# Reordering TensorE's step lists in a transformer kernel of two branches

## The chip, the cores and the metric

The kernel runs on one core of one Trainium2 chip. The metric is the device time of one execution in microseconds (us); the figure for the kernel before is the median of three runs. A core has five engines with an instruction queue each: TensorE (PE in the profile; its weight loads are shown apart as PEld), VectorE (DVE), ScalarE (ACT), GpSimd (POOL) and SyncE (SP), which here issues the transfers. Each queue is worked off in the order in which it was written, and engines wait for each other through semaphores.

## The reference

The input x has 8 batches of 512 tokens with 128 features. It is layer-normalised once, and two branches work on the result; their sum is added to x.

```
x  = L0_attn_x                     # (8, 512, 128)
xn = _layernorm(x)
x  = x + attention(xn) + layers(xn)

attention: 16 heads of 8, causal, with a relative-position term of 5 rows for k and for v
layers:    for i in range(6):
               x = local_attn(shift_tokens(x)) + x
               x = ffn(shift_tokens(x)) + x

local_attn(x): q, k, v = split(x @ Wqkv)          # 16 heads of 64
               q, k = l2norm(q) * qs, l2norm(k) * ks, then rotary with a scale
               windows of 32: queries of a window see its keys and those of the window before
               softmax, then @ v, then @ Wo
ffn(x):        xn = layernorm(x) * g + b
               a, gate = split(xn @ W1 + b1)      # 2 x 341 columns
               a * gelu(gate) @ W2 + b2
```

## The kernel before

The first part, up to about 460 us of the profiled span, is the relative attention. The change does not touch it. The second part, from there to the end, is the six layers. It walks over 6 x 8 x 4 = 192 tiles of 128 tokens (layer, batch, quarter of the batch); n is a tile's number. A tile's place in its batch is called tile 0, 1, 2 or 3 below, and four tiles of one batch are a stretch.

Work on a tile is cut into named steps, which functions inside `steps_of_layers` emit. They are pipelined over tiles: while tile n has its scores made, tile n + 2 is projected and tile n - 1 is attended to.

- `p0` to `p3` (`project`, L776): a product of three matmuls (high and low halves of 32-bit numbers, L670 to L672) into `qk_ps`. VectorE multiplies it by the rotary cosine (L799) and sine (L800), ScalarE squares it (L801). After `p1` and `p3`, GpSimd adds the two rotary parts (L806). After `p1` it also adds the squares (L808), which VectorE sums per head (L809); after `p3` VectorE sums the squares directly (L811).
- `r` (`normalise`, L816): a chain of nine small VectorE instructions (L821, L75 to L86) on a tile `root_ps`, then GpSimd scales q and k (L826).
- `q0 q1 k0 k1` (`turn`, L840): four transposes each into `qkT_ps` (L845) and a ScalarE copy (L848).
- `s0 s1` (`scores`, L850): into two banks `sc_ps` a mask (L867) and 64 small matmuls (L879). VectorE takes two row maxima (L888), ScalarE eight exponentials (L892). After `s1`, VectorE inverts the sums (L904), GpSimd scales the probabilities (L905) and VectorE turns them into `pT` (L907).
- `v0` to `v3` (`values`, L912): a product into `v_ps`, a ScalarE copy (L921) and four transfers on SP's queue (L923).
- `a0 a1` (`attend`, L928): small matmuls into `y_ps` (L941), and after `a1` a ScalarE copy `ys` (L952). `+` (`add`, L955) turns `ys` and VectorE adds it to the stream `xt` (L962).
- `f`: one piece of the feed-forward of a batch that is complete. A stretch holds nine: split and mean (L976) in tile 1 after `+`, variance in tile 2, `rstd` in tile 3, then in the next tile 0 the three gate products with three Gelu activations (L1032) and three value products (L1042), and in the next tile 1 the last product `f_ps` (L1054), which VectorE adds to `xt` (L1066).
- `w1 w2`: pieces of the next layer's joint v and output weights. They do something only in tiles 2 and 3 of a layer's last batch.

The order of TensorE's instructions is written by hand: the strings of `ORDERS` (L49 to L54), one for each place in the batch, are read word by word (L1162). On the other engines the framework's scheduler sets a fixed order when the program is built, from its own estimates of times. So a change of `ORDERS` can also change the fixed order of the other four queues.

All products, turnings and the small chains take their PSUM tiles from one pool of six banks (`ps_x`, L1128). The scores have two banks of their own. A step that is given a bank waits until the step that had it before has been read out. Which bank a step gets is fixed at build time too. Exponentials and Gelu belong to different activation tables, so that each stretch has two table loads on ScalarE.

Of the kernel before, what the change touches and what calls it, by code (L numbers as in the profile page):

```python
# [46 lines left out]


ORDERS = (  # L49
    "p0 p1 v0 f s0 w2 + p2 f p3 q0 f f q1 s1 w2 k0 v1 w1 a0 r a1 w1 k1 v2 v3",  # L50
    "p0 s0 w2 p1 p2 v0 q0 f p3 f + f q1 s1 w2 k0 v1 w1 a0 r a1 w1 k1 v2 v3 f",
    "p0 p1 s0 w2 v0 v1 f p2 q0 q1 p3 s1 w2 k0 w1 + a0 r a1 w1 k1 v2 v3",
    "p0 p1 s0 w2 v0 f p2 q0 + q1 p3 v1 s1 w2 k0 w1 a0 r a1 w1 k1 v2 v3",
)  # L54


# [1230 lines left out]
```

## Time and profile before

| | |
|---|---|
| median of three runs | 3420.91 us (3416.99 to 3425.21) |
| profiled execution, its own time | 3422.36 us |
| span of the profiled execution | 3420.6 us |
| TensorE clock granted, mean | 0.992 |
| busy share PE / DVE / ACT / POOL | 94% / 88% / 81% / 80% |
| exponentials L892, without their accumulator reads | 3072, mean 348 ns |
| rotary products L799 and L800 | 768 each, mean 681 and 678 ns |
| table loads on ScalarE (L1032 and L892) | 47 and 46, mean 1283 ns |

The busy share of TensorE is from modelled ends of pipelined matmuls, so it is no proof that TensorE sets the time. The last column of a group's line tells how long the engine stood idle before these instructions, and what ended the wait. In a timeline, a line has the start, the duration, the engine, the line of the kernel, what is written and read, and in brackets the idle time before it with what ended it.

### The profile page before, as it was taken

Reading aid. Unit: us, or ns where it says so; the run is one execution under the profiler, and the core shown is the slowest. Engines: PE = TensorE matmul, PEld = TensorE weight load, DVE = VectorE, ACT = ScalarE, POOL = GpSimd, SP = SyncE. Lnnn points to the kernel's source line nnn. Section 1 sums busy time; section 2 is a strip of 40 time slices with the busy share of each in tenths; the row PEclk is TensorE's granted clock in tenths of the full one; section 3 lists DMA queues with packets and bytes.
Section 4 is the critical chain, followed back from the end, with each engine's and each line's share of the span. In section 5 each row is a group of like instructions: output and inputs, shape, how many; then the busy total and the mean of one; then the engine's idle time right before and its main releaser. Section 6 shows DMA issues by size and latency. Waiting matters only on the chain.

```text
span 3420.6 us, 132912 instructions
## 1 busy us (share of the span) xinstructions
PE 3207.7 (94%) x51264; PEld 2394.4 (70%) x51264; DVE 2998.4 (88%) x7542; ACT 2783.2 (81%) x9786; POOL 2752.1 (80%) x2102
## 2 busy tenths in 40 slices
PE   7999979999999999999999999999999999999997
PEld 4667657777777777667777767777767777776775
DVE  7777788999999999899898998989999898998994
ACT  5777768888888888888888888888888888887884
POOL 6767668888888888788888888888888887887883
PEclk9999999999999999999999999999999999999998
DMA  2111123332333323333233332323333233332332
GB/s 59 37 40 46 48 72 74 75 73 72 89 82 78 74 71 79 84 87 75 69 75 78 83 87 69 77 70 86 82 80 76 69 78 77 81 80 75 83 75 58
DMA packets 221067, 250.07 MB, mean 73 GB/s; under 512 B 73238, under 2 KB 115604, under 8 KB 220436
## 3 DMA queue, kind: packets, MB, share of 16 engines
q1 hardware_dynamic: 220148, 241.18, 28.4%
q8 instruction: 407, 6.67, 0.9%
q14 instruction: 224, 1.84, 0.2%
q10 hardware_dynamic: 288, 0.39, 0.1%
HBM read 26.92 MB, written 4.19 MB: 9 GB/s over the span
## 4 chain that ended last, share of the span: by engine, by line
PE 43%; DVE 27%; ACT 18%; issue 4%; DMA 3%; POOL 3%; SPq 2%; ACTq 0%; POOLq 0%; DVEq 0%
ACT pr L892 8%; PE y_ps L941 8%; PE qkT_ps L845 6%; PE sc_ps L879 4%; DVE q L799 4%; DVE rot L800 4%; PE f_ps L1054 3%; PE v_ps L670 2%; PE v_ps L671 2%; PE v_ps L672 2%; ACT sq L801 2%; DVE pT L907 2%; DVE mx L888 2%; PE qk_ps L670 2%; ACT L892 2%
## 5 line engine op out<-in xcount | busy, mean ns | idle before, releaser
L892 ACT ACTIVATE pr<-sc_ps,mx 128x64 f32<-128x64 f32 x3072 | 923.4, 348 | 96.9 <-DVE mx L888 92.6
L806 POOL TENSOR_TENSOR q<-q,rot 128x1024 f32<-128x1024 f32 x380 | 924.8, 2434 | 91.8 <-DVE rot L800 62.9
L826 POOL TENSOR_TENSOR q<-q,rn 128x1024 f32<-128x1024 f32 x380 | 717.4, 1909 | 4.1 <-DVE rn L86 3.8
L892 ACT ACTIVATION_READ_ACCUMULATOR pr<-sc_ps,mx 128x1 f32 x3072 | 719.5, 241 | 0.0
L801 ACT ACTIVATE sq<-qk_ps 128x512 f32<-128x512 f32 x768 | 469.7, 633 | 262.1 <-DVE rot L800 157.6
L905 POOL TENSOR_TENSOR pr<-pr,sm 128x1024 f32<-128x1024 f32 x192 | 365.7, 1905 | 337.9 <-DVE rn L86 188.7
L799 DVE TENSOR_TENSOR q<-qk_ps,wrot 128x512 f32<-128x512 f32 x768 | 523.1, 681 | 48.1 <-PE qk_ps L672 43.3
L800 DVE TENSOR_TENSOR rot<-qk_ps,wrot 128x512 f32<-128x512 f32 x768 | 520.6, 678 | 0.0
L921 ACT COPY v<-v_ps 128x512 f32<-128x512 f32 x768 | 469.7, 660 | 48.8 <-PE v_ps L672 21.9
L845 PE MATMUL qkT_ps<-ident,q 128*128 128x128 f32 x3072 | 480.0, 282 | 24.8 <-POOL q L826 15.0
L845 PEld LDWEIGHTS qkT_ps<-ident,q 128*128 128x128 f32 x3072 | 340.3, 141 | 148.4 <-POOL q L826 58.0
L879 PEld LDWEIGHTS sc_ps<-kT,qT 64*32 64x32 f32 x24576 | 272.8, 105 | 183.2 <-issue 182.4
L941 PE MATMUL y_ps<-vw,pT 128*32 128x128 f32 x11904 | 382.0, 275 | 2.8 <-DMA vw<-v 2.8
L941 PEld LDWEIGHTS y_ps<-vw,pT 128*32 128x32 f32 x11904 | 327.6, 110 | 57.5 <-issue 28.5
L670 PE MATMUL qk_ps<-wqk_hi,xs_hi 128*128 128x512 f32 x768 | 347.1, 452 | 5.9 <-ACT sq L801 2.5
L670 PE MATMUL v_ps<-wvo_hi,xs_hi 128*128 128x512 f32 x768 | 338.8, 441 | 7.3 <-ACT ys L952 6.2
L879 PE MATMUL sc_ps<-kT,qT 64*32 64x64 f32 x24576 | 335.5, 225 | 0.0
L672 PE MATMUL qk_ps<-wqk_hi,xs_lo 128*128 128x512 f32 x768 | 304.5, 396 | 0.9 <-POOL xs_lo L659 0.9
L672 PE MATMUL v_ps<-wvo_hi,xs_lo 128*128 128x512 f32 x768 | 304.1, 396 | 0.0
L671 PE MATMUL qk_ps<-wqk_lo,xs_hi 128*128 128x512 f32 x768 | 303.7, 395 | 0.0
L671 PE MATMUL v_ps<-wvo_lo,xs_hi 128*128 128x512 f32 x768 | 302.7, 394 | 0.0
L888 DVE TENSOR_REDUCE mx<-sc_ps 128x4 f32<-128x256 f32 x768 | 282.4, 407 | 10.7 <-PE sc_ps L879 9.0
(206 smaller groups left out, 7058.9 us busy)
## 6 DMA issues: line engine op xcount, KB each, us to landing
vw<-v SPq DMA_DIRECT2D x3072, 64.0 KB
a_qz<-a_qT SPq DMA_DIRECT2D x128, 64.0 KB
wqk_raw<-in_Wqk SPq DMA_DIRECT2D x24, 256.0 KB
wv_raw<-in_WvT SPq DMA_DIRECT2D x12, 256.0 KB
wo_raw<-in_Wo SPq DMA_DIRECT2D x12, 256.0 KB
wrot<-in_trig SPq DMA_DIRECT2D x24, 128.0 KB
a_x<-in_x SPq DMA_DIRECT2D x8, 256.0 KB
a_res<-in_x SPq DMA_DIRECT2D x8, 256.0 KB
```

What stands on the lines that cost most here:

```text
L670: nc.tensor.matmul(ps, lhsT=ah, rhs=bh, start=True, stop=False)
L671: nc.tensor.matmul(ps, lhsT=ah, rhs=bl, start=False, stop=False)
L672: nc.tensor.matmul(ps, lhsT=al, rhs=bh, start=False, stop=True)
L799: nc.vector.tensor_mul(q[:, :, a], ps, wide(cos[:, a, :]))
L800: nc.vector.tensor_mul(v[:, :, 1 - a], ps, wide(sin[:, 1 - a, :]))
L801: nc.scalar.activation(sq[:, a], ps, AF.Square)
L806: adds.tensor_add(q, q, v)
L826: scales_by.tensor_mul(q, q, r[:, m, :].unsqueeze(2).to_broadcast([P, H, D]))
L845: nc.tensor.transpose(tr[:, m, :], q[:, 2 * hp : 2 * hp + 2, :].rearrange("p h d -> p (h d)"), ident)
L879: nc.tensor.matmul(ps[32 * j : 32 * j + 32, w, :], lhsT=qT[r, 4 * g + j, W * w : W * w + W], rhs=kT[r, 4 * g + j, W * w : W * w + 2 * W], ...
L892: nc.scalar.activation(pr[:, p, g, w, :], ps[:, w, :], AF.Exp, bias=mx[:, p, g, w : w + 1], accum_out=sm[:, m : m + 1],),
L941: nc.tensor.matmul(y[W * w : W * w + W, :], lhsT=pT[:, p, g, w, half, :], rhs=v[:, p, g, :], start=(p, g, half) == (0, 0, 0 if keys[w] is ...
```

## The change

Only `ORDERS` changes. No step is added or removed.

```
-    "p0 p1 v0 f s0 w2 + p2 f p3 q0 f f q1 s1 w2 k0 v1 w1 a0 r a1 w1 k1 v2 v3",
-    "p0 s0 w2 p1 p2 v0 q0 f p3 f + f q1 s1 w2 k0 v1 w1 a0 r a1 w1 k1 v2 v3 f",
-    "p0 p1 s0 w2 v0 v1 f p2 q0 q1 p3 s1 w2 k0 w1 + a0 r a1 w1 k1 v2 v3",
-    "p0 p1 s0 w2 v0 f p2 q0 + q1 p3 v1 s1 w2 k0 w1 a0 r a1 w1 k1 v2 v3",
+    "f p0 p1 v0 w2 s0 + p2 f p3 q0 f f q1 s1 w2 k0 v1 w1 a0 r a1 w1 v2 v3 k1",
+    "p0 w2 s0 p1 p2 v0 f q0 p3 f + f q1 s1 w2 v1 k0 w1 a0 r a1 w1 v2 v3 k1 f",
+    "p0 p1 s0 v0 v1 f w2 p2 q0 w2 q1 p3 s1 k0 w1 + a0 r a1 w1 v2 v3 k1",
+    "p0 p1 w2 s0 v0 f p2 q0 + q1 p3 v1 s1 w2 k0 w1 a0 r w1 v2 v3 a1 k1",
```

Leaving out the `w` steps, which do nothing in most tiles, this comes to: in tile 0 the gate products stand before `p0` instead of after `v0`; in tile 1 the last feed-forward product stands before `q0` and `v1` before `k0`; in every tile `k1` stands after `v3`; in tile 3 `a1` also stands after `v3`. In the last batch of a layer the first piece of the joint weights is made in tile 2 after the variance instead of after `s0`.

## The prediction

> **What bounds the kernel now.** I read the page first, then the chain of waits' releasers, then the timeline of one stretch without a change of layer, engine by engine. The page:
>
> ```profile
> PE 3207.7 (94%) x51264; PEld 2394.4 (70%) x51264; DVE 2998.4 (88%) x7542; ACT 2783.2 (81%) x9786; POOL 2752.1 (80%) x2102
> ...
> PE 43%; DVE 27%; ACT 18%; issue 4%; DMA 3%; POOL 3%; SPq 2%; ACTq 0%; POOLq 0%; DVEq 0%
> ```
>
> TensorE looks like the bound, but three engines share the chain. The view of who waited for whom says where TensorE stands and why:
>
> ```profile
> ACT sq L801 <- DVE rot L800: 157.6, 217, 3.3
> PE sc_ps L867 <- ACT pr L892: 84.9, 136, 1.6
> DVE xt L1066 <- PE f_ps L1054: 45.5, 44, 6.7
> PEld mean_ps L976 <- ACT v L921: 28.3, 40, 1.7
> ```
>
> In each line: total, times, longest. TensorE waits for the banks that the exponentials hold, and before the mean (L976) for a bank that a copy of v holds. VectorE waits about 1 us in nearly each stretch for `f_ps`. Who is late is seen in a stretch that begins (`p0` of tile 0) at 1672.15 and lasts 59.53 us:
>
> ```profile
> 1674.05 0.19 DVE L86 SCALAR_TENSOR_TENSOR rn<-root_ps,rn 128x32 f32<-128x32 f32 x1
> 1673.38 1.91 POOL L905 TENSOR_TENSOR pr<-pr,sm 128x1024 f32<-128x1024 f32 x1 [1.59 <-DVE root_ps L82]
> ...
> 1675.54 0.60 ACT L801 ACTIVATE sq<-qk_ps 128x512 f32<-128x512 f32 x1 [0.26 <-DVE rot L800]
> 1679.78 1.28 ACT L892 ACT_TABLE_LOAD   x1
> 1683.61 0.27 PE L867 MATMUL sc_ps<-masks,ident_b 128*128 128x256 bf16 x1 [0.92 <-ACT pr L892]
> 1685.53 1.22 DVE L811 TENSOR_REDUCE ss<-sq 128x16 f32<-128x1024 f32 x1 [1.00 <-ACT sq L801]
> ...
> 1693.85 0.66 PE L845 MATMUL qkT_ps<-ident,q 128*128 128x128 f32 x4
> 1694.34 2.74 PE L1054 MATMUL f_ps<-h,w 128*128 128x512 f32 x6
> 1697.12 1.51 DVE L1066 SCALAR_TENSOR_TENSOR xt<-f_ps,wg,xt 64x512 f32<-64x512 f32 x2 [0.88 <-PE f_ps L1054]
> 1701.20 0.76 DVE L888 TENSOR_REDUCE mx<-sc_ps 128x4 f32<-128x256 f32 x2
> 1701.87 1.21 DVE L811 TENSOR_REDUCE ss<-sq 128x16 f32<-128x1024 f32 x1
> 1703.98 0.62 ACT L921 COPY v<-v_ps 128x512 f32<-128x512 f32 x1
> 1704.44 0.32 ACT L952 COPY ys<-y_ps 128x128 f32<-128x128 f32 x1
> 1704.65 0.50 PE L976 MATMUL mean_ps<-fx_hi,ones 128*128 128x512 f32 x1
> 1705.22 0.40 PE L670 MATMUL qk_ps<-wqk_hi,xs_hi 128*128 128x512 f32 x1
> ```
>
> The path: from 1672.4 to 1683.5 ScalarE sets the time. It works with 0.26 us of idle from the last exponentials of the tile before, through both table loads, to the exponentials of `s0`. They free the bank for which TensorE waits (0.92), and VectorE waits 1.00 us for the square behind them. From there TensorE runs without a hole to `f_ps`, for which VectorE waits 0.88. From 1697.1 on VectorE is the bound: up to the next tile 0 its timeline shows only waits of 0.16 and 0.24 us. So a stretch is ScalarE, then TensorE, then VectorE, and an edit pays only on its piece of this path.
>
> **The change part by part.** The order of the other queues in the built kernels, read beside the diff, is part of the change.
>
> *Edit 1, gates ahead of `p0`, tile 0 (48 stretches).* The nine gate matmuls (0.23 us start to start) move; none is added. ScalarE's work up to `s0`'s exponentials is the same list in another order: Gelu x3, the copy of v, both squares, the load, the exponentials. So only its idle 0.26 can go: they start at 1681.08, 1.30 after the load, and could at 1680.82. But VectorE's queue changes too: `pT` now stands ahead of all four rotary products. It needs GpSimd's product, which ends at 1673.38 + 1.91 = 1675.29, while VectorE is done with L86 at 1674.24: a new wait of 1.05. Then `pT` (1.16 to the next start), four products at 0.60, the last one lasting 0.68, end at 1675.32 + 1.16 + 1.80 + 0.68 = 1678.96. The second square now stands ahead of the load, and the trace has a square 0.10 after its product: 1679.06 + 0.60 + 1.30 (load and start) = 1680.96. The later of both counts: a gain of 0.12. I take 0.15, since the two paths end within 0.15 of each other. The cover of the 1.05 is VectorE's own later wait of 1.00 and one of 0.44 before it; if that cover is gone, the wait is paid. Bounds: 0.26 gained at best (the idle), 0.5 lost at worst (half the new wait). TensorE meets new bank waits (the second gate for a copy of v, the third for the root tile, free at 1674.24, together about 0.7), but its `s0` would end near 1678.2, and VectorE gets to those maxima only at 1678.96: hidden.
>
> *Edit 2, `f_ps` ahead of `q0`, tile 1.* The four transposes take 1694.34 - 1693.85 = 0.49 and now stand behind. VectorE's wait for `f_ps` shrinks by 0.49 and by the gain of edit 1, which TensorE carries here without a hole: together g = 0.64, below the 0.88 there is. `q0`'s copy comes 2.2 us later; its reader is `s0` of the next tile, over 10 us away.
>
> *Edit 3, `v1` ahead of `k0`, tile 1.* With `k1` at the end, the mean gets the bank of `k0`, whose copy stands ahead of the exponentials, instead of that of `v1`, whose copy stood behind them. This wait of TensorE goes (28.3 us in all). What is late next: `p0` of tile 2 has the bank of `y_ps`, free after `ys`. `ys` loses the copy of v ahead of it, but the scheduler also put VectorE's sum L811 ahead of the maxima of `s1`, which costs these 1.15 (as 1685.53 to 1686.67). Sum: the exponentials ended at 1704.04; + 1.15 - g, + 0.26 for `ys`, + 0.05 to TensorE = 1705.50 - g, against 1705.22. So the stretch gains g - 0.28 = 0.36, and nothing at g = 0.28. The mean and VectorE's chain of nine are done by then. Bounds for the three edits together: a loss of 0.28 (g = 0, edit 1 at its worst) and a gain of 0.60 (g = 0.88, all of VectorE's wait).
>
> *Edit 4, `k1` to the end, and `a1` behind `v3` in tile 3.* The turning takes 0.41 of TensorE either way. The copies of v and their eight SP transfers come earlier, that of k later by some 1.4; its reader `s1` is more than 7 us away, and the y products have waited 2.8 us in all for v's transfers. `ys` in tile 3 comes about 1.5 later; `+` reads it over 3 us later in the profile. Taken at 0; without this cover, up to a copy's 0.67 us.
>
> *Edit 5, the `w` steps.* Five times, the joint weights come 2.4 us later in tile 2; the first copy of their high half no longer stands ahead of `s0`'s exponentials on ScalarE. Bounds of plus and minus 1 us each, taken at 0: 5 us both ways.
>
> From tile 2 to the end of tile 3 VectorE's queue holds the same work back to back and carries the gain to the next stretch. Sum: 47 full stretches x 0.36 = 17 us. The profiled execution took 3422.4, so 3405.4; the median of the runs is 1.4 lower: **3404 us**.
>
> A page that speaks against it: the Trainium skill, "Perfetto Trace Analysis", Identifying the Most-Contended Engine, advises to judge VectorE, ScalarE and GpSimd by occupancy and to improve the most occupied first, and not to trust matmul busy time. That names VectorE (88%), whose work the change leaves alone, and the sum by it would be 0, 3421 us. The rows above, with 0.88 and 1.00 us of VectorE idle per stretch, are why I don't follow it.
>
> **The rivals.**
> - *The gain is eaten.* The sum L811 ahead of the maxima costs 1.15, and g is only about 0.3. For it: 0.49 alone leaves just 0.21, less 0.05 at each handing over. Time: 3417 to 3424.
> - *Slower: the new wait for GpSimd in tile 0.* VectorE stands 1.05 us ahead of `pT`, and ScalarE's squares, now ahead of the load, hand all further delay to the exponentials. It decides when these start after 1681.29 (g under 0.28). At edit 1's lower bound g is 0 and a stretch loses 0.28: 13 us, 3434. Squares a whole microsecond later make g = -0.36 and 3451. For it: both paths end within 0.15. Against it: GpSimd is idle 1.59 ahead of its product, so nothing but the sums holds it.
> - *More gain.* TensorE's bank waits go as well (84.9 us for exponentials in all) and the changes of layer gain. With 1.0 us a stretch, 47 us: 3374. Against it: VectorE's later pieces have no idle to give.
>
> **How the numbers follow.** Forecast (3394 to 3413): 0.46. More gain (3374 to 3394): 0.17. Eaten: 0.17, almost all of it within 7 us (0.2%, about what a measurement of this kernel tells from no change). Slower: 0.20. Range: from 3378, a little above the lowest case, to 3432, near the slower case. Faster 0.63, same 0.17, slower 0.20.
>
> **What the next profile would show.** The wait of the mean for ScalarE's copy of v (28.3) nearly gone: edit 3. VectorE's wait for `f_ps` falling from 45.5 to about 20: edit 2. A VectorE wait near 1 us ahead of `pT` in tile 0, and that of L811 for squares shrinking: edit 1. Wrong if the first exponentials of tile 0 start more than 8.93 us (now 1681.08 - 1672.15) after the stretch's first matmul, or if VectorE shows new idle in tiles 2 and 3.

## The result and the profile after

The changed kernel is slower: 3440.76 us median of four runs (3437.33 to 3442.66) beside 3421.7 for the kernel before, a ratio of 1.0055 with a 95% interval of 1.0039 to 1.0071. The forecast was 3404, faster. The profiled execution took 3442.66 us with a span of 3440.9, at a granted clock of 0.988 (before 0.992). The lower clock does not explain it: two kernels below with a still lower one, `a_lo_first` (mean 0.987) and `a_lo_first_v1_late` (0.986), are faster than the change.

The page of the kernel after, busy times and chain:

```profile
PE 3234.3 (94%) x51264; PEld 2397.0 (70%) x51264; DVE 3041.7 (88%) x7542; ACT 2784.7 (81%) x9786; POOL 2757.8 (80%) x2102
...
PE 46%; DVE 21%; POOL 12%; ACT 12%; DMA 4%; issue 3%; SPq 2%; POOLq 0%; ACTq 0%; DVEq 0%
```

Two numbers stand out. VectorE is busy 43 us longer (2998.4 to 3041.7) with the same 7542 instructions, and GpSimd's share of the chain went from 3% to 12%. Now who waited for whom, the kernel after (total, times, longest):

```profile
DVE pT L907 <- POOL pr L905: 56.1, 60, 2.1
PE sc_ps L867 <- ACT pr L892: 59.4, 120, 1.3
DVE ss L809 <- POOL sq L808: 24.8, 44, 0.9
DVE xt L1066 <- PE f_ps L1054: 17.6, 39, 6.4
DVE ss L811 <- ACT sq L801: 6.0, 27, 0.9
```

These are nearly the signs that the prediction asked for. The wait of the mean for the copy of v (28.3 before) has gone from the list, VectorE's wait for `f_ps` fell from 45.5 to 17.6, that of L811 from 46.5 to 6.0, and the new wait ahead of `pT` is there, 1.07 in the stretch below. What the prediction did not name is VectorE's wait for GpSimd's sum of squares (L809), which grew from 15.2 to 24.8 and moved: before, 10.3 us of it (34 of 43 times) stood in tile 0 and 2.5 (5 times) in tile 2; after, 20.9 (36 of 44 times) stand in tile 2. New idle of VectorE in tile 2 was one of the prediction's two signs of being wrong. (The other did not come: the first exponentials of tile 0 start 8.36 after the first matmul of the stretch, not over 8.93.) So the change did on TensorE what it was to do, and the time still rose.

Where it rose is seen from marks. Each is the mean over 20 stretches in the middle of the layers 0 to 4, in us from the end of the last exponentials of the stretch before:

| mark | before | after | change |
|---|---|---|---|
| first exponentials of tile 0 | 8.53 | 8.19 | -0.34 |
| `f_ps` done, tile 1 | 24.53 | 23.58 | -0.95 |
| maxima of `s1`, tile 1 | 28.65 | 28.83 | +0.18 |
| first rotary product, tile 2 | 33.58 | 32.98 | -0.60 |
| third of the four cosine products L799, tile 2 | 38.47 | 37.87 | -0.60 |
| sum L809, tile 2 | 41.33 | 41.43 | +0.10 |
| maxima of `s1`, tile 2 | 41.99 | 42.12 | +0.13 |
| first rotary product, tile 3 | 47.17 | 47.78 | +0.61 |
| end of the stretch | 59.47 | 60.12 | +0.65 |

Up to tile 2 the gain is there, and larger than the 0.36 forecast. Between the first products of tile 2 and of tile 3, 1.2 us are lost: 0.70 up to the sum L809, the other 0.51 behind it. The timeline of one stretch of the kernel after (its first matmul starts at 1681.66; the stretch shown of before began at 1672.15), first up to `f_ps`, then VectorE, GpSimd and two copies of ScalarE through tiles 1 and 2:

```profile
1682.52 1.91 POOL L905 TENSOR_TENSOR pr<-pr,sm 128x1024 f32<-128x1024 f32 x1 [1.58 <-DVE root_ps L82]
1684.45 1.25 DVE L907 STREAM_TRANSPOSE pT<-pr 128x1024 f32<-128x1024 f32 x1 [1.07 <-POOL pr L905]
1688.72 1.28 ACT L892 ACT_TABLE_LOAD   x1
1692.54 0.27 PE L867 MATMUL sc_ps<-masks,ident_b 128*128 128x256 bf16 x1 [0.37 <-ACT pr L892]
1694.47 1.22 DVE L811 TENSOR_REDUCE ss<-sq 128x16 f32<-128x1024 f32 x1
...
1702.62 2.74 PE L1054 MATMUL f_ps<-h,w 128*128 128x512 f32 x6
1705.40 1.52 DVE L1066 SCALAR_TENSOR_TENSOR xt<-f_ps,wg,xt 64x512 f32<-64x512 f32 x2 [0.22 <-PE f_ps L1054]
1709.29 0.58 ACT L921 COPY v<-v_ps 128x512 f32<-128x512 f32 x1
1709.36 1.21 DVE L811 TENSOR_REDUCE ss<-sq 128x16 f32<-128x1024 f32 x1
1709.76 0.59 ACT L848 COPY kT<-qkT_ps 128x512 f32<-128x512 f32 x1
1710.60 0.76 DVE L888 TENSOR_REDUCE mx<-sc_ps 128x4 f32<-128x256 f32 x2
1713.57 0.26 DVE L904 RECIPROCAL sm<-sm 128x16 f32<-128x16 f32 x1 [0.27 <-ACT pr L892]
1713.97 1.91 POOL L905 TENSOR_TENSOR pr<-pr,sm 128x1024 f32<-128x1024 f32 x1 [2.16 <-DVE rn L86]
...
1721.88 1.27 POOL L808 TENSOR_TENSOR sq<-sq 128x512 f32<-128x512 f32 x1
1723.19 0.69 DVE L809 TENSOR_REDUCE ss<-sq 128x16 f32<-128x512 f32 x1 [0.27 <-POOL sq L808]
1724.11 0.76 DVE L888 TENSOR_REDUCE mx<-sc_ps 128x4 f32<-128x256 f32 x2 [0.15 <-PE sc_ps L879]
...
1726.67 0.19 DVE L821 TENSOR_SCALAR root_ps<-ss 128x32 f32<-128x32 f32 x1
1726.89 0.17 DVE L996 CAST rstd_hi<-rstd 128x4 fp32r<-128x4 f32 x1
1727.14 1.04 POOL L1002 TENSOR_TENSOR dg<-ident,rstd_hi 128x512 fp32r<-128x512 f32 x1 [1.66 <-DVE rstd_hi L996]
1727.20 1.00 DVE L997 TENSOR_TENSOR rstd_lo<-rstd,rstd_hi 128x4 fp32r<-128x4 f32 x1
```

Three orders that the scheduler chose, and that the diff does not name, differ from before in most stretches:

- **The sum.** In tile 1 VectorE takes the sum L811 (1709.36) ahead of the maxima L888 (1710.60). The prediction knew this and priced it on TensorE's path. But the exponentials behind the maxima also feed L904 and GpSimd's L905 (1713.97), and from there GpSimd works without a hole through both scalings L826, the addition L806 and the squares L808, until 1723.15. VectorE waits for that at 1723.19.
- **The rest.** In tile 2 VectorE's tiny L997 (the low part of `rstd`, 128 x 4) starts 0.06 behind GpSimd's product `dg`, and takes 1.00 us.
- **The copy.** In tile 2 ScalarE copies `v1` ahead of the exponentials of `s0`, and waits there for a transfer that still reads the copy's buffer. The total of such waits ("v" for "vw<-v" ahead of L921, all tiles) is 18.5 us beside 15.8 before, but now the exponentials stand behind it: their first start has a standard deviation of 0.59 us over the 20 stretches, 0.09 before.

In the last layer the two kernels can be compared with these orders alike: there the kernel before has all three itself, in batches 2 to 5 of 0 to 7, and the changed kernel's stretch is the shorter in three of these four and the same in one (60.74, 60.79, 61.35 and 60.78 us beside 61.59, 63.96, 61.35 and 61.53). From the last exponentials of layer 4 to the end the profiled execution gained 7.9 us (536.1 to 528.2); up to there it lost 28.3.

The second order is best seen in one line's instructions, before and after; it gives shortest, median and longest duration in ns. First the kernel before:

```profile
L997 DVE TENSOR_TENSOR rstd_lo<-rstd,rstd_hi x48: 157/164/999, 563.0 to 3400.1; 128x4 fp32r<-128x4 f32 x48
```

The kernel after:

```profile
L997 DVE TENSOR_TENSOR rstd_lo<-rstd,rstd_hi x48: 161/999/1198, 560.8 to 3421.3; 128x4 fp32r<-128x4 f32 x48
```

The median is six times as long. All 48 together took 12.8 us before and 47.2 after, 34 of the 43 us by which VectorE is busier. No list of waits shows it, since the profile has it as busy time. In the kernel before, the same two instructions met the other way round by 0.04 us:

```profile
1717.23 1.04 POOL L1002 TENSOR_TENSOR dg<-ident,rstd_hi 128x512 fp32r<-128x512 f32 x1 [0.55 <-DVE rstd_hi L996]
...
1716.98 0.17 DVE L996 CAST rstd_hi<-rstd 128x4 fp32r<-128x4 f32 x1
1717.06 0.19 DVE L821 TENSOR_SCALAR root_ps<-ss 128x32 f32<-128x32 f32 x1
1717.19 0.16 DVE L997 TENSOR_TENSOR rstd_lo<-rstd,rstd_hi 128x4 fp32r<-128x4 f32 x1
```

The Trainium skill, "SBUF — State Buffer", Who interferes with whom, says that a VectorE instruction with two inputs in SBUF contends with a GpSimd instruction that reads SBUF, that the ports they share are an exclusive lock, and that issue order decides who blocks. The lines agree for L997: it reads two SBUF tiles, and 1727.20 + 1.00 is 0.02 behind the end of `dg` at 1727.14 + 1.04, as in all 41 stretches of the change in which it starts 0.06 behind `dg`. That GpSimd is held in its turn no line here shows: `dg` takes 1.04 behind L997 as well.

### The profile page after: what moved, and what is told of

It reads as the page before. It is cut to its first block, busy times and chain, and to the rows that moved or that the text cites. A ratio compares the mean times of both kernels' runs of the same rounds, so it can differ in the third digit from the quotient of the medians.

```text
span 3440.9 us, 133114 instructions
## 1 busy us (share of the span) xinstructions
PE 3234.3 (94%) x51264; PEld 2397.0 (70%) x51264; DVE 3041.7 (88%) x7542; ACT 2784.7 (81%) x9786; POOL 2757.8 (80%) x2102
## 3 DMA queue, kind: packets, MB, share of 16 engines
q1 hardware_dynamic: 220148, 241.18, 28.3%
## 4 chain that ended last, share of the span: by engine, by line
PE 46%; DVE 21%; POOL 12%; ACT 12%; DMA 4%; issue 3%; SPq 2%; POOLq 0%; ACTq 0%; DVEq 0%
PE y_ps L941 7%; ACT pr L892 6%; PE qkT_ps L845 5%; POOL q L826 4%; PE sc_ps L879 4%; PE v_ps L670 4%; PE f_ps L1054 3%; PE v_ps L671 3%; POOL q L806 3%; POOL pr L905 3%; PE v_ps L672 2%; PE qk_ps L670 2%; DMA vw<-v 2%; DVE rot L800 2%; DVE q L799 2%
## 5 line engine op out<-in xcount | busy, mean ns | idle before, releaser
L806 POOL TENSOR_TENSOR q<-q,rot 128x1024 f32<-128x1024 f32 x380 | 924.9, 2434 | 57.4 <-DVE rot L800 51.4
L826 POOL TENSOR_TENSOR q<-q,rn 128x1024 f32<-128x1024 f32 x380 | 721.3, 1919 | 0.6 <-DVE rn L86 0.6
L892 ACT ACTIVATION_READ_ACCUMULATOR pr<-sc_ps,mx 128x1 f32 x3072 | 704.4, 234 | 0.0
L905 POOL TENSOR_TENSOR pr<-pr,sm 128x1024 f32<-128x1024 f32 x192 | 365.6, 1904 | 374.5 <-DVE rn L86 267.4
L799 DVE TENSOR_TENSOR q<-qk_ps,wrot 128x512 f32<-128x512 f32 x768 | 524.1, 682 | 61.2 <-PE qk_ps L672 56.2
L845 PE MATMUL qkT_ps<-ident,q 128*128 128x128 f32 x3072 | 466.8, 278 | 50.2 <-POOL q L826 35.9
L921 ACT COPY v<-v_ps 128x512 f32<-128x512 f32 x768 | 463.6, 636 | 34.8 <-DMA vw<-v 18.5
L845 PEld LDWEIGHTS qkT_ps<-ident,q 128*128 128x128 f32 x3072 | 359.4, 141 | 169.7 <-POOL q L826 65.3
L941 PE MATMUL y_ps<-vw,pT 128*32 128x128 f32 x11904 | 390.2, 275 | 1.5 <-DMA vw<-v 1.5
L670 PE MATMUL v_ps<-wvo_hi,xs_hi 128*128 128x512 f32 x768 | 347.2, 452 | 0.2 <-issue 0.2
L907 DVE STREAM_TRANSPOSE pT<-pr 128x1024 f32<-128x1024 f32 x192 | 238.1, 1240 | 58.8 <-POOL pr L905 56.1
```

What stands on the lines that cost most here:

```text
L670: nc.tensor.matmul(ps, lhsT=ah, rhs=bh, start=True, stop=False)
L799: nc.vector.tensor_mul(q[:, :, a], ps, wide(cos[:, a, :]))
L806: adds.tensor_add(q, q, v)
L826: scales_by.tensor_mul(q, q, r[:, m, :].unsqueeze(2).to_broadcast([P, H, D]))
L845: nc.tensor.transpose(tr[:, m, :], q[:, 2 * hp : 2 * hp + 2, :].rearrange("p h d -> p (h d)"), ident)
L892: nc.scalar.activation(pr[:, p, g, w, :], ps[:, w, :], AF.Exp, bias=mx[:, p, g, w : w + 1], accum_out=sm[:, m : m + 1],),
```

## The experiments

The theories are: **S**, the stall of L997 takes the gain; **D**, the copy of `v1` ahead of the exponentials does; **G**, the new wait ahead of `pT` does; and, formed after the first four runs, **P**, the sum ahead of the maxima delays GpSimd's chain, and that delays VectorE in tile 2. The table has all runs, the stretch being the last mark of the table above (before: 59.47).

| run | built on | median, us | ratio to before, 95% | stretch, us |
|---|---|---|---|---|
| the change | | 3440.8 | 1.0055 (1.0039 to 1.0071) | 60.12 |
| a_lo_first | after | 3434.5 | 1.0022 (1.0013 to 1.0031) | 59.69 |
| a_v1_late | after | 3443.5 | 1.0041 (1.0028 to 1.0053) | 60.08 |
| a_lo_first_v1_late | after | 3431.1 | 1.0010 (1.0001 to 1.0019) | 59.52 |
| b_lo_first | before | 3430.1 | 1.0008 (0.9999 to 1.0017) | 59.70 |
| a_mx | after | 3413.0 | 0.9964 (0.9952 to 0.9977) | 59.56 |
| a_mx_lo | after | 3399.7 | 0.9922 (0.9908 to 0.9936) | 59.09 |
| b_sum_lo_v1 | before | 3458.3 | 1.0098 (1.0084 to 1.0112) | 60.44 |
| p_gates | before | 3414.1 | 0.9968 (0.9955 to 0.9980) | 59.36 |
| p_fy | before | 3438.1 | 1.0033 (1.0021 to 1.0045) | 60.29 |
| p_k1 | before | 3443.0 | 1.0048 (1.0036 to 1.0061) | 59.95 |
| a_mx_rest | after | 3399.9 | 0.9921 (0.9908 to 0.9934) | 59.22 |
| gf_mx_rest | before | 3381.9 | 0.9867 (0.9855 to 0.9880) | 58.75 |
| n3 | after | 3385.8 | 0.9890 (0.9877 to 0.9904) | 58.80 |
| n4 | after | 3409.4 | 0.9961 (0.9948 to 0.9973) | 59.28 |
| n5 | after | 3400.7 | 0.9927 (0.9913 to 0.9941) | 59.21 |

The runs were made in four groups, each with its own runs of the kernel before (medians 3426.4, 3426.3, 3426.9 and 3423.9), so differences between groups are read from the ratios.

### The stall and the copy

In `a_lo_first` GpSimd makes the low half's product first. This product needs L997, so it can't run beside it:

```
         dg = [p3.tile([P, NT, P], F32R, name="dg", tag="h", bufs=3) for _ in range(2)]
-        for n in range(2):
+        for n in (1, 0):
             nc.gpsimd.tensor_mul(
```

> The changed kernel with one line different: GpSimd makes the second of its two diagonal tiles (of rstd's low half, L1002) first, so that VectorE's subtraction L997 always ends before GpSimd begins. Theory S (VectorE's small subtraction L997 stands behind GpSimd's first product, because both read SBUF, and its 47 us of duration are on VectorE's path): L997 falls from 47.2 us to 8 to 13, and the kernel from 3440.8 to 3406 to 3418. Theory D (the copy of v1 in tile 2 waits for transfers ahead of the exponentials): no change, 3437 to 3443. Theory G (VectorE's new wait for GpSimd ahead of pT in tile 0, 48 us): no change, 3437 to 3443.

In `a_v1_late` the copy of `v1` in tile 2 is ordered behind the exponentials of `s0` on ScalarE:

```
-        ecopy(VAR['v'][j])(v, ps)
+        copied = ecopy(VAR['v'][j])(v, ps)
+        if t == 2 and j == 1:
+            tc.add_manual_dep(
+                copied.ins,
+                last["any"].name,
...
```

> The changed kernel with the copy of v1 in tile 2 put behind the exponentials of s0 on ScalarE, as it stood in the kernel before; nothing else is asked for. Theory D: the idle time ahead of this copy (21.2 us against 6.0 before) goes and the kernel gains 10 to 15 us, 3426 to 3431. Theory S: L997 stays at about 47 us and the kernel at 3435 to 3443. Theory G: no change, 3437 to 3443.

`a_lo_first_v1_late` has both edits, and `b_lo_first` is the kernel before with the first edit.

> Both edits in the changed kernel. Theories S and D, if both hold and add up: 3392 to 3408, which is faster than the kernel before (3421.7). S alone: 3406 to 3418, as with the first edit alone. D alone: 3426 to 3431. G: 3437 to 3443.

> The kernel before with the same one line different. Its L997 lasts 12.8 us in all, since only 6 of 48 fall behind GpSimd. Theory S: a gain of at most 5 us, 3416 to 3424. If the other order of GpSimd's products is better by itself, whatever L997 does, this kernel gains as much as the changed one does.

In `a_lo_first` L997 is back at 0.15 us (the columns are as above):

```profile
L997 DVE TENSOR_TENSOR rstd_lo<-rstd,rstd_hi x48: 150/152/1199, 562.0 to 3415.6; 128x4 fp32r<-128x4 f32 x48
```

The time fell by 0.33%, 0.43 us a stretch. So S is real and falls short: the kernel is still 0.22% slower than before, far from the 3406 to 3418 that S alone gave. The cure also has a price of its own. With it the first exponentials of tile 0 come 0.21 later in the changed kernel (8.40) and 0.15 later in the kernel before (`b_lo_first`, 8.68), which took 1.0008 and a stretch of 59.70 where 3416 to 3424 was expected. Why is not known; it makes the 0.33% a low figure for the stall. D alone gave 0.14%, inside the two intervals, and 0.04 us a stretch, less than expected. Moving the copy brings the first exponentials of tile 2 forward (37.54 to 37.01) but leaves the maxima of `s1` in tile 2 where they were (42.12 to 42.10), so something else held these. G falls with `p_gates` below, which has the wait ahead of `pT` (43.3 us in all, 7.9 before) and is faster than before. With both cures the time was 0.10% above before, where 3392 to 3408 was expected. 0.6% of the forecast (1.0010 beside 3404 / 3421.7, 0.995) was still missing, and the marks gave the place: between the maxima of `s1` in tiles 1 and 2, with GpSimd without a hole. That made theory P.

### The place of the sum

`a_mx` puts one order back. The sum L811 of the last tile of a batch is emitted behind the maxima of `s1` in tile 1 (the last two lines stand in `scores`), and ordered behind them:

```
-            nc.vector.tensor_reduce(
-                ss[:, part, :], sq.rearrange("p a h d -> p h a d"), AX.XY, ALU.add
-            )
+            def total(after=None):
+                summed = nc.vector.tensor_reduce(
+                    ss[:, part, :], sq.rearrange("p a h d -> p h a d"), AX.XY, ALU.add
+                )
+                if after is not None:
+                    tc.add_manual_dep(
+                        summed.ins,
+                        after.ins.name,
...
+            if t == 3:
+                put_off.append(total)
+            else:
+                total()
...
+        while put_off:
+            put_off.pop()(maxima)
```

> The changed kernel with one order put back: in tile 1 VectorE takes the maxima of s1 ahead of the sum L811, as it did before the change (the sum is emitted behind the maxima; nothing else is edited). Theory P (the sum delays the exponentials, they delay GpSimd's chain from L905 to L808, and that delays VectorE in tile 2): the maxima of s1 in tile 1 start about 1.1 us earlier (28.8 to 27.7 from the start of the stretch), those of tile 2 start 0.5 to 1.1 earlier, a stretch falls from 60.1 to 59.0 to 59.6, and the time from 3441 to between 3392 and 3418. Rival T (TensorE's banks set tile 2, GpSimd only looks late): the maxima of tile 1 come earlier but those of tile 2 stay, 3436 to 3444. The wait of L997 for GpSimd stays about 1 us in either.

`a_mx_lo` has the low half first as well.

> The same with GpSimd's product of the low half first as well. Theory P with theory S (the stall of L997 costs by itself): a stretch of 58.5 to 59.2 us and 3372 to 3403. Rival T: no better than the low half first alone, 3430 to 3436. Rival: the two waits hide each other, so that the second cure brings under 3 us on top of the first.

`b_sum_lo_v1` is the reverse on the kernel before: both maxima of `s1` in tile 1 are ordered behind that sum, with the low half first and the copy late.

> The kernel before with the sum L811 forced ahead of both maxima of s1 in tile 1, the low half's product first, and the copy of v1 in tile 2 behind the exponentials of s0, so that of the changed kernel's three new orders only the sum's is there. Theory P: before had no slack there, so all of the sum's 1.15 us is lost in each stretch: 60.3 to 60.7 us, 3465 to 3490. Rival T: 3424 to 3436, as the kernel before with the low half first.

All three came out as P said in sign and stretch. Putting the maxima first took 0.9% off the changed kernel (1.0055 to 0.9964), and 1.33% with the low half first (to 0.9922, 26.6 us below before). Forcing the sum first cost the kernel before 0.9% (1.0008 to 1.0098). In the last case the time was 7 us under the range. In the built `a_mx` the copy of `v1` was back behind the exponentials in 41 of the 46 stretches in which the change had it ahead, without being asked to, so `a_mx_lo` has all three orders of before in nearly every stretch. The timeline of `a_mx` (its stretch begins at 1667.05; L901 are the maxima, L920 GpSimd's scaling of the probabilities):

```profile
1694.20 0.69 DVE L809 TENSOR_REDUCE ss<-sq 128x16 f32<-128x512 f32 x1
1694.92 0.76 DVE L901 TENSOR_REDUCE mx<-sc_ps 128x4 f32<-128x256 f32 x2
...
1698.29 1.90 POOL L920 TENSOR_TENSOR pr<-pr,sm 128x1024 f32<-128x1024 f32 x1 [1.03 <-DVE rn_s L81]
...
1706.34 1.29 POOL L808 TENSOR_TENSOR sq<-sq 128x512 f32<-128x512 f32 x1
1708.18 0.68 DVE L809 TENSOR_REDUCE ss<-sq 128x16 f32<-128x512 f32 x1
```

GpSimd starts on the probabilities 31.24 after the start of the stretch (32.31 in the change), and L809 of tile 2 no longer starts as GpSimd's squares end: 1706.34 + 1.29 = 1707.63, and L809 at 1708.18. The maxima of tile 1 came 1.12 earlier, those of tile 2 only 0.52: GpSimd's chain gave up its place after half a microsecond. That the sum's place decides is shown, once each way. That its delay reaches VectorE through GpSimd is read from these lines; no run changed GpSimd's work alone.

### Parts of the change alone

`p_gates` is edit 1 on the kernel before, `p_fy` edit 2, and `p_k1` edit 4 without the move of `a1` (in all four lists; the list of tile 2 is shown):

```
-    "p0 p1 v0 f s0 w2 + p2 f p3 q0 f f q1 s1 w2 k0 v1 w1 a0 r a1 w1 k1 v2 v3",
+    "f p0 p1 v0 s0 w2 + p2 f p3 q0 f f q1 s1 w2 k0 v1 w1 a0 r a1 w1 k1 v2 v3",
...
-    "p0 s0 w2 p1 p2 v0 q0 f p3 f + f q1 s1 w2 k0 v1 w1 a0 r a1 w1 k1 v2 v3 f",
+    "p0 s0 w2 p1 p2 v0 f q0 p3 f + f q1 s1 w2 k0 v1 w1 a0 r a1 w1 k1 v2 v3 f",
...
-    "p0 p1 s0 w2 v0 v1 f p2 q0 q1 p3 s1 w2 k0 w1 + a0 r a1 w1 k1 v2 v3",
+    "p0 p1 s0 w2 v0 v1 f p2 q0 q1 p3 s1 w2 k0 w1 + a0 r a1 w1 v2 v3 k1",
```

> The kernel before with the gates ahead of p0 in tile 0 alone (edit 1 of the prediction). The prediction's step: 0.15 us a stretch, 7 us, 3414 to 3421 beside 3422 to 3426 of before; the wait ahead of pT of about 1.05 shows and is hidden. Theory P gives the same, as tile 1's maxima stay ahead of the sum and come 0.15 earlier. Rival (the new wait costs): 3430 or more.

> The kernel before with f_ps ahead of q0 in tile 1 alone (edit 2 of the prediction). In the built kernel this edit by itself puts the sum L811 ahead of the maxima of s1 in tile 1, the low half's subtraction L997 behind GpSimd's product, and the copy of v1 in tile 2 ahead of the exponentials. The prediction's step: a gain of 0.49 us a stretch, 3400 to 3410. Theory P with S (the planner's new orders cost more than the edit gives): maxima of tile 1 at 28.65 - 0.49 + 1.15 = 29.3 us of the stretch, the stretch at 60.1 to 60.9, 3450 to 3480.

> The kernel before with k1 at the end of each tile alone (edit 4 without the move of a1). Of the three new orders the built kernel has only that of L997 behind GpSimd's product. The prediction's step: 0, 3418 to 3426. Theory S (the stall pays by itself, also with the maxima first): the stall of L997 near 1 us shows, a stretch takes 59.8 to 60.0 and the time is 3435 to 3448. Rival: without the sum ahead of the maxima the stall falls in time that is spare, and the time is as before.

Edit 1 alone makes the kernel faster, 0.32%, a little above what was expected of it. The stretch gained 0.11 us; the wait ahead of `pT` shows and costs nothing. Edits 2 and 4 alone make it slower. Edit 2 does bring `f_ps` 0.81 earlier (23.72 beside 24.53), and by itself turns all three orders; the stretch lost 0.82, as expected, but the time lay 12 us below the range that this gave. Of this, the last batches of the first five layers gained 8 us (from one batch's last exponentials to the next's, 304.9 beside 313.1), and the last layer, where before has these orders too, lost nothing. Edit 4 turns only the order of L997, with the maxima still first, and that alone costs 0.48%. Its L997 (columns as above):

```profile
L997 DVE TENSOR_TENSOR rstd_lo<-rstd,rstd_hi x48: 157/998/1003, 562.6 to 3423.9; 128x4 fp32r<-128x4 f32 x48
```

So S holds by itself too: the stretch is 0.48 us longer, of the 0.83 that the instruction grew. The place of `k1` is the other thing that this run changes, but its marks up to tile 2 are all 0.1 ahead of before, and the loss comes behind L809 of tile 2 (41.22 beside 41.33), where L997 stands.

### The orders held, and the edits priced

`a_mx_rest` holds both orders on the changed kernel in another way than with the low half first. The maxima come first as in `a_mx`, and VectorE's next root stands behind L997:

```
-        nc.vector.tensor_scalar_max(x, ss.rearrange("p m h -> p (m h)"), 1e-24)
+        floored = nc.vector.tensor_scalar_max(x, ss.rearrange("p m h -> p (m h)"), 1e-24)
+        if rest:
+            tc.add_manual_dep(
+                floored.ins,
+                rest.pop().ins.name,
...
-        nc.vector.tensor_sub(parts[1], rstd, parts[0].bitcast(F32))
+        rest[:] = [nc.vector.tensor_sub(parts[1], rstd, parts[0].bitcast(F32))]
```

`gf_mx_rest` has the same orders held, on the kernel before with edits 1 and 2 only.

> The changed kernel with the maxima of s1 ahead of the sum in tile 1, and with VectorE's next root (L821) put behind L997, so that L997 stands ahead of GpSimd's product, whose halves keep their order. All three new orders are then undone. Theory: as with the low half first, but without the 0.15 us that this cost in tile 0: a stretch of 58.8 to 59.0 us and 3388 to 3400. Rival: the low half first was needed as such, 3405 to 3413.

> The kernel before with edits 1 and 2 alone (gates ahead of p0, f_ps ahead of q0) and the same two orders held: maxima ahead of the sum, L997 ahead of the root. Beside the run with all five edits it prices edits 3 to 5. The prediction's steps: edit 3 saves 0.3 (the wait of the mean), edits 4 and 5 nothing, so 10 to 20 us slower than the run with all edits: 3400 to 3415. Rival: the mean's wait was never on the path once the maxima come first: within 5 us of it.

`a_mx_rest` took what `a_mx_lo` took. Beside `a_mx` it prices the stall without the other cure's cost: 0.43%, 0.34 us a stretch. It kept the 0.13 us in tile 0, but its maxima of `s1` in tile 3 came 0.6 later, so the stretch was 59.22 and not under 59.0. `gf_mx_rest` fell outside both expectations: 18 us faster than with all five edits, 1.33% faster than before (0.9867, 0.9855 to 0.9880), the fastest kernel of this study. Not all of that is the edits: no run holds the orders on the kernel before, which has them the other way in the last layer, and there the profiled execution gained 14.9 of its 40.3 us. In the regular stretch, where before has the held orders, edits 1 and 2 gain 0.72 us (59.47 to 58.75). Edits 3 to 5 together cost 18 us once the orders are held. Three runs each leave one of them out of `a_mx_rest`: `n3` edit 3, `n4` edit 4 (in all four lists), `n5` edit 5 (in all four). One list of each:

```
-    "p0 w2 s0 p1 p2 v0 f q0 p3 f + f q1 s1 w2 v1 k0 w1 a0 r a1 w1 v2 v3 k1 f",
+    "p0 w2 s0 p1 p2 v0 f q0 p3 f + f q1 s1 w2 k0 v1 w1 a0 r a1 w1 v2 v3 k1 f",
...
-    "p0 p1 w2 s0 v0 f p2 q0 + q1 p3 v1 s1 w2 k0 w1 a0 r w1 v2 v3 a1 k1",
+    "p0 p1 w2 s0 v0 f p2 q0 + q1 p3 v1 s1 w2 k0 w1 a0 r a1 w1 k1 v2 v3",
...
-    "p0 p1 s0 v0 v1 f w2 p2 q0 w2 q1 p3 s1 k0 w1 + a0 r a1 w1 v2 v3 k1",
+    "p0 p1 s0 w2 v0 v1 f p2 q0 q1 p3 s1 w2 k0 w1 + a0 r a1 w1 v2 v3 k1",
```

> The changed kernel with both orders held (maxima ahead of the sum, L997 ahead of the root), without edit 3: k0 ahead of v1 in tile 1 again. With all five edits held so it took 3399.9, with edits 1 and 2 alone 3381.9. Theory (edit 3 is the cost: the mean gets the bank of k0, whose copy now stands behind the exponentials and behind that of v1): the mean starts 0.2 us earlier, tile 2 with it by 0.3 to 0.5, 3382 to 3390. Rival (the late k1 is the cost): 3396 to 3404.

> The same without edit 4 instead: k1 ahead of v2 and v3 again, a1 ahead of them in tile 3. Rival theory (the late k1 and the late a1 are the cost, as ScalarE's last copy and GpSimd's next work come later): 3382 to 3390. Theory that edit 3 alone costs: 3396 to 3404. If both cost, each run lies between, 3388 to 3396.

> The same without edit 5 instead: the steps w where they stood. The prediction's step (5 us at most, either way, since it occurs at the five changes of layer only): 3395 to 3405. If the joint weights are the cost: 3382 to 3390, all of it in the stretches next to a change of layer, and the regular stretch stays 59.2.

Edit 3 costs: without it the ratio goes from 0.9921 to 0.9890, the stretch from 59.22 to 58.80, and the mean starts 0.52 earlier (31.18 beside 31.70 from the last exponentials of the stretch before). Edit 5 is nothing (0.9927). Without edit 4 the kernel is 0.40% slower, 5 us above the highest figure expected; its regular stretch is only 0.06 longer, and most of the loss lies near the changes of layer and at the end, which I did not follow. The rest between `n3` and `gf_mx_rest`, 0.23%, does not lie in the regular stretch, which differs by 0.05; the last batches of the first five layers take 319.2 us in `n3` and 311.7 in `gf_mx_rest`, but the two profiled executions are only 2.0 us apart. This too stays open.

What edit 3 does is seen on ScalarE and TensorE at the end of tile 1. In `a_mx_rest` (stretch from 1662.87; L943 copies v, L865 are the transposes, L998 the mean):

```profile
1693.48 0.62 ACT L943 COPY v<-v_ps 128x512 f32<-128x512 f32 x1
1693.95 0.65 ACT L868 COPY kT<-qkT_ps 128x512 f32<-128x512 f32 x1
1694.16 0.42 PEld L865 LDWEIGHTS qkT_ps<-ident,q 128*128 128x128 f32 x4 [0.53 <-ACT v L943]
1694.16 0.66 PE L865 MATMUL qkT_ps<-ident,q 128*128 128x128 f32 x4
...
1694.64 0.50 PE L998 MATMUL mean_ps<-fx_hi,ones 128*128 128x512 f32 x1
```

In `n3` (from 1656.53):

```profile
1684.12 0.58 ACT L868 COPY kT<-qkT_ps 128x512 f32<-128x512 f32 x1
...
1687.10 0.62 ACT L943 COPY v<-v_ps 128x512 f32<-128x512 f32 x1
1687.27 0.59 PEld L865 LDWEIGHTS qkT_ps<-ident,q 128*128 128x128 f32 x4
1687.50 0.60 PE L865 MATMUL qkT_ps<-ident,q 128*128 128x128 f32 x4
...
1687.85 0.48 PE L998 MATMUL mean_ps<-fx_hi,ones 128*128 128x512 f32 x1
```

The copy of `v1` stands behind the exponentials in both. With edit 3, `k1` gets the bank that it holds, waits 0.53 for it, and the mean stands behind `k1`. Without edit 3 `k1` gets the bank of `k0`, whose copy was made at 1684.12, ahead of the exponentials, and the copy of `v1` is out of its bank as the mean comes to need it. The wait that edit 3 took from the mean went to a step ahead of it.

## Why the prediction was wrong

**The step that failed** is "From tile 2 to the end of tile 3 VectorE's queue holds the same work back to back and carries the gain to the next stretch." The gain was there in tile 2 (0.60 at its first and third cosine products, forecast 0.36) and at the first product of tile 3 it was a loss of 0.61. The work was the same, but neither its order nor its durations were, and VectorE was not alone on the path.

- *Same work.* The scheduler put L997 behind GpSimd's product, and its 0.16 us became 1.00. The prediction compared the orders of the queues only around the edits. Cured, this is worth 0.33% in the change and 0.43% with the maxima first, and it costs 0.48% in `p_k1`, where it is the only order that turns.
- *VectorE carries.* In the kernel before, VectorE hardly ever waits for GpSimd's squares in tile 2 (5 times), but L809 starts there 0.09 us behind their end on average, and 0.03 where it waits. GpSimd's chain from the exponentials of tile 1 to this sum had some 0.06 us of slack. So VectorE could come to the sum earlier only if GpSimd did, and GpSimd's squares ended 0.15 later than before (41.39 beside 41.24). In the stretch of before that the prediction showed:

```profile
1712.50 1.28 POOL L808 TENSOR_TENSOR sq<-sq 128x512 f32<-128x512 f32 x1
...
1713.79 0.16 DVE L84 TENSOR_TENSOR root_ps<-root_ps,rstd 128x4 f32<-128x4 f32 x1
1713.86 0.68 DVE L809 TENSOR_REDUCE ss<-sq 128x16 f32<-128x512 f32 x1
```

The squares end at 1713.78, and L809 starts at 1713.86. I followed the 1.15 us of the sum L811 along ScalarE and TensorE, where its cost came out as worked out (the maxima +0.18, and 1.15 - 0.95 is 0.20), and not along the branch from the exponentials to GpSimd.

**With the three orders of before,** the forecast's stretch is met: `a_mx_lo` gained 0.38 us a regular stretch where 0.36 was forecast. The agreement is in part luck, as edit 3 then costs and edits 1 and 2 give more. In all it gained 0.78% where 0.5% was forecast, but 12 of the 20 us by which its profiled execution is shorter lie in the last layer, where the kernel before has the orders of the change.

**Edit 1** was right in kind and too small. The sum gave 0.15. Alone it brought the exponentials 0.21 earlier, `f_ps` 0.19 and the stretch 0.11. The cover of the new wait ahead of `pT` held. The whole change shows 0.34 at the exponentials, above the bound of 0.26. Two other edits, alone, also bring something there, 0.13 (`p_k1`) and 0.14 (`p_fy`), which the prediction credited to neither; and edits 1 and 2 with the orders held bring 0.37 without the move of `k1` (`gf_mx_rest`). Why is not shown.

**Edit 2** was mis-sized. It was put at 0.49 for the transposes; alone it brought `f_ps` 0.81 earlier, 0.14 of it before the exponentials of tile 0. In the whole change `f_ps` came 0.95 earlier, where g was put at 0.64 and at most at 0.88.

**Edit 3** was wrong in its reason. "This wait of TensorE goes" is true only while the sum holds back the exponentials, so that both copies stand ahead of them (1709.29 and 1709.76). With the maxima first the wait stands at `k1`, and the edit costs 0.3%.

**Edit 4** was "Taken at 0". Alone it costs 0.48% through the order of L997; beside edit 3, with the orders held, it is worth 0.40%. The prediction's 2.8 us of waits for v's transfers counted TensorE's products only; their weight loads had 4.6 more. **Edit 5** at 0 was right (0.06%, inside the intervals).

**The rivals.** "The gain is eaten" named the right instruction, the sum ahead of the maxima, but on TensorE's path, where the 0.95 by which `f_ps` came earlier nearly paid for it; its range ended at 3424. The slower one gave 3434 to 3451, and the time fell in it, but by another cause: the wait for GpSimd in tile 0 was hidden as forecast, and the one that counted was in tile 2. The page that was weighed in the prediction named VectorE by its occupancy. The first chain shown here ran through TensorE in tiles 0 and 1, and edits 1 and 2 there gain 0.72 us a regular stretch with the orders held; but it was VectorE's order that decided whether this was seen.

## What to carry to other kernels

Where a scheduler orders the other queues, a change of one engine's list is a change of all of them: compare the whole order of each queue in the built kernel, tile by tile, and not only around the edit. When a maximum, a sum or a copy moves on a shared engine, follow every consumer to the next place where some engine waits, and look in the timeline of before for readers that start just as their producer ends, since such a chain has no slack and no list of waits shows it. Price the edits again with the orders held by hand: here five edits that lose 0.55% as built hold two that, with the orders held, make a kernel 1.33% faster than before.

## What the runs showed of the hardware that I had not expected

A VectorE instruction of 128 x 4 elements with two SBUF inputs took 0.15 to 0.17 us alone, and 1.00 us when it started 0.06 us behind a GpSimd product of 1.04 us: 41 of 48 cases in the change, each ending 0.02 behind the product. Five more took 1.19 to 1.20, started 0.10 to 0.12 behind GpSimd's squares L808 (1.27 to 1.29). The blocked time is booked as busy, so no list of waits shows it; the only signs are a median of six times the shortest duration, and 34 us more busy time for the same 48 instructions. In the 42 cases of the kernel before in which it started 0.04 to 0.11 us ahead of the product, it took 0.16 to 0.17.
